# A deformable layer with tiles of 2 by 8 pixels: hats turned once, written to memory and read back as weights

## The chip, the cores and the metric

The kernel runs on one core of a Trainium2 chip. All values are float32. The metric is the device time of one execution in microseconds (us). Before the change three runs took 5849.1, 5850.1 and 5858.9 us; the median is 5850.1.

## The reference

The input x has shape (2, 128, 128, 128): image, channel, row, column. Four layers follow one another, each as x + layer(group_norm(x)): an attention along columns (layer 0), four recurrent scans (layer 1), a deformable convolution (layer 2) and a 4 by 4 Hadamard convolution (layer 3). The change is in layer 2:

```python
out = conv2d(x, w_off, b_off)              # 27 values per pixel
offset = out[:, :18]                       # 9 taps, (y, x)
mask = jax.nn.sigmoid(out[:, 18:])         # 9 taps
py = off_y + ky + hh                       # where tap k reads
px = off_x + kx + ww
sampled = v00*(1-wy)*(1-wx) + v01*(1-wy)*wx + v10*wy*(1-wx) + v11*wy*wx
sampled = sampled * mask
out = einsum('bckhw,ock->bohw', sampled, w) + b
```

So each output pixel reads, for each of 9 taps, the normalised image at a place that is not whole, by bilinear interpolation. The weight of a source pixel at distance (dy, dx) from that place is hat(dy) hat(dx), with hat(d) = max(0, 1 - |d|). A sum over a small window of source pixels, weighted by products of hats, is the same as the interpolation when no offset is larger than the window allows.

## The kernel before

Layer 2 has two stages. `layer2_offsets` (L1123) goes through the images in blocks of 16 rows, 8 per image. For each block it normalises the rows (ACT, L1167), computes the 27 offset and mask channels with 36 products (L1179), turns them so that pixels lie on partitions (om L1187, pt L1195, ot L1199) and writes them to memory as `off_d` (L1203). It also turns the normalised image, so that columns lie on partitions and channels in the free dimension (px L1211, xt L1212), and writes it to memory as `px_d` (L1213), a picture with a border of three pixels of zeros that ACT's queue has written before (L1143, L1148). A last step tests the largest offset: if it is over 2, a slow general way is taken (`layer2_gather`), which does not run here. All engines read that flag and branch (L1116).

`layer2_windows` (L1231) does the sampling. Its unit is a half: 4 rows by 64 columns, 256 pixels, cut into 16 tiles of 4 by 4 pixels. There are 128 halves. A tile's pixels read from a window of 10 by 10 source pixels, which lie on 100 partitions of `xw`, one 128-channel row per tile. The steps for a half:

- `load` (L1253): SP issues ten transfers, one for each window row (L1263), each with 10 columns x 16 tiles x 512 B, and one for the offsets `o` (L1265).
- `hats` (DVE), `hatted` (ACT, absolute value and relu) and `masked` (DVE): for each pixel and tap the ten hats along y and the ten along x, the y ones times the mask.
- `outer` (DVE): for 128 pixels, the products of hats, `w` with 9 taps x 100 places. `turn` (PE): nine transposes of 128 by 100 through the identity, into `ps_w`. `turned` (DVE): copy to `s`, so that each tile has 9 taps x 16 pixels = 144 columns.
- `sample` (PE): eight products for each 128 pixels, `xw` of the tile (100 x 128) with `s` of the tile (100 x 144). A float32 product appears in the trace as two records. `sampled` (ACT): three copies to `sm`.
- `convolve` (PE): nine products with `wdef`, 128 x 128 with 256 columns. `finish` (DVE): adds bias and residual into `res`, and for every second half the statistics of the next norm.

The order on PE, DVE and ACT is the order in which the code calls them: the wrapper `InOrder` (L73) keeps it, so that nearly all of these instructions carry its line, L81. In iteration b of the loop PE runs `turn` of the next 128 pixels, `sample` of these, then `convolve` of the half before (five taps, then four). DVE runs the copy `s`, the outer product for two steps ahead, the hats or the masking for two halves ahead, and `finish`. Loads are asked for three halves ahead, `xw` has four buffers, `ps_w` and `ps_s` one. SP is not wrapped; it issues its transfers one after another, and one that waits holds all that follow.

Of the kernel before, what the change touches and what calls it, by code (L numbers as in the profile page):

```python
# [7 lines left out]
F32 = mybir.dt.float32  # L8
I32 = mybir.dt.int32
AF = mybir.ActivationFunctionType  # L10
ALU = mybir.AluOpType
# [4 lines left out]
P = 128  # L16
N = 2
S = 128
RT = 4
NT = S // RT  # L20
# [4 lines left out]
TP = S + 6  # L25
TE = 131
# [1096 lines left out]
def layer2_offsets(env, prm, res, mem, st_gn, far):  # L1123


    nc, tc = env.nc, env.tc
    ident = env.ident
    NR = 16
    with ExitStack() as ctx:
        cp = ctx.enter_context(tc.tile_pool(name="l2c", bufs=1))  # L1130
# [6 lines left out]
        zero = cp.tile([P, 402], F32, name="zero", tag="zero")  # L1137
        nc.vector.memset(zero, 0.0)
        for n in range(N):
            flat = mem["px"][n].rearrange("y x k -> (y x k)")  # L1140
            for y in (0, S + 3):
                span = 3 * TP * P
                nc.scalar.dma_start(  # L1143
                    out=flat[y * TP * P : y * TP * P + span].rearrange("(p k) -> p k", p=P),
                    in_=zero,
                )
            for c in (0, S + 3):
                nc.scalar.dma_start(  # L1148
                    out=mem["px"][n, 3 : S + 3, c : c + 3, :].rearrange("y x k -> y (x k)"),
                    in_=zero[:, 0 : 3 * P],  # L1150
                )
# [7 lines left out]
        for n in range(N):  # L1159
            for h in range(0, S, NR):  # L1160
# [15 lines left out]
                for k in range(9):  # L1176
# [9 lines left out]
                om = sp.tile([P, 4, RT, 32], F32, name="om", tag="om")  # L1186
                nc.scalar.activation(  # L1187
                    om.rearrange("p b r c -> p r b c"),
                    ps.rearrange("p r (b c) -> p r b c", b=4),
                    AF.Identity,  # L1190
                    bias=boff,
                )
# [15 lines left out]
                for q in range(0, NR, RT):  # L1208
# [4 lines left out]
                nc.sync.dma_start(  # L1213
                    out=mem["px"][n, h + 3 : h + 3 + NR, 3 : S + 3, :].rearrange("y x k -> x y k"),
                    in_=xt,
                )
# [14 lines left out]
def layer2_windows(env, prm, res, mem, st_next):  # L1231
# [3 lines left out]

    nc, tc = env.nc, env.tc
    ident = env.ident
    with ExitStack() as ctx:
# [3 lines left out]
        pe, dve, act = (InOrder(tc, e) for e in (nc.tensor, nc.vector, nc.scalar))  # L1242
# [4 lines left out]
        base = cp.tile([P, 18, 10], F32, name="base", tag="base")  # L1247
        nc.scalar.dma_start(out=base, in_=prm["base2"])

        px = mem["px"]  # L1250
        halves = [(n, g, hf) for n in range(N) for g in range(NT) for hf in range(2)]

        def load(at):  # L1253
            n, g, hf = halves[at]
            xw = sp.tile([100, 16, P], F32, name="xw", tag="xw", bufs=4)
            for y in range(10):
                here = px[n, g * RT + y, hf * 64 : hf * 64 + 10, :]
                src = bass.AP(
                    tensor=here.tensor,
                    offset=here.offset,  # L1260
                    ap=[[P, 10], [4 * P, 16], [1, P]],
                )
                nc.sync.dma_start(out=xw[10 * y : 10 * y + 10], in_=src)  # L1263
            o = sp.tile([P, 2, 27], F32, name="o", tag="o", bufs=4)
            nc.sync.dma_start(out=o, in_=mem["off"][n, g, :, 2 * hf : 2 * hf + 2, :])  # L1265
            return xw, o

        def hats(o):
            d = sp.tile([P, 2, 18, 10], F32, name="d", tag="d")
            dve.tensor_tensor(  # L1270
                d,
                o[:, :, 0:18].unsqueeze(3).to_broadcast([P, 2, 18, 10]),
                base.unsqueeze(1).to_broadcast([P, 2, 18, 10]),
                ALU.add,
            )
            return d

        def hatted(d):
            act.activation(d, d, AF.Abs)
            act.activation(d, d, AF.Relu, bias=1.0, scale=-1.0)  # L1280

        def masked(d, o):
            rows = d.rearrange("p b (k a) s -> p b k a s", a=2)[:, :, :, 0, :]
            dve.tensor_tensor(
                rows, rows, o[:, :, 18:27].unsqueeze(3).to_broadcast([P, 2, 9, 10]), ALU.mult
            )

        def outer(d, b):
            w = sp.tile([P, 9, 10, 10], F32, name="w", tag="w")
            v = d[:, b].rearrange("p (k a) s -> p k a s", a=2)  # L1290
            dve.tensor_tensor(
                w,
                v[:, :, 0, :].unsqueeze(3).to_broadcast([P, 9, 10, 10]),
                v[:, :, 1, :].unsqueeze(2).to_broadcast([P, 9, 10, 10]),
                ALU.mult,
            )
            return w

        def turn(w):
            ps = pp.tile([100, 9, P], F32, name="ps_w", tag="ps_w")  # L1300
            for k in range(9):
                pe.transpose(ps[:, k, :], w[:, k].rearrange("p y x -> p (y x)"), ident)
            return ps

        def turned(ps):

            s = sp.tile([100, 8, 36, 4], F32, name="s", tag="s")
            dve.tensor_copy(
                s.rearrange("p t k c -> p k t c"),
                ps.rearrange("p k (r t c) -> p (k r) t c", r=4, t=8),  # L1310
            )
            return s
# [13 lines left out]
        def sampled(ps, sm, b):  # L1326
            for j in range(3):
                nt = (3, 3, 2)[j]
                lo = 8 * b + 3 * j
                act.copy(  # L1330
                    sm.rearrange("p k (t c) -> p k t c", c=4)[:, :, lo : lo + nt, :],
                    ps[:, j, 0 : nt * 144].rearrange("p (t k c) -> p k t c", t=nt, c=4),
                )

        def convolve(sm, po, taps):
            for k in taps:
                pe.matmul(
                    po,
                    lhsT=wdef[:, k, :],
                    rhs=sm[:, 4 * k : 4 * k + 4, :],  # L1340
                    start=(k == 0),
                    stop=(k == 8),
                )

        def finish(at, po):
            n, g, hf = halves[at]
            here = res[n][:, g * RT : g * RT + RT, hf * 64 : hf * 64 + 64]
            dve.scalar_tensor_tensor(here, po, bdef[:, 0:1], here, ALU.add, ALU.add)
            if hf == 1:
                dve.bn_stats(  # L1350
                    st_next[:, n, g, :],
                    res[n][:, g * RT : g * RT + RT, :].rearrange("p h w -> p (h w)"),
                )

        count = len(halves)
        loads = {at: load(at) for at in range(3)}
        ds = {}
        for at in range(2):  # L1360
            ds[at] = hats(loads[at][1])
            hatted(ds[at])
            masked(ds[at], loads[at][1])
        w = outer(ds[0], 0)
        ps_w = turn(w)
        s = turned(ps_w)
        w = outer(ds[0], 1)
        sms, pos = {}, {}
        for b in range(2 * count + 2):
            at, part = b // 2, b % 2  # L1370
            if part == 0 and at + 3 < count:
                loads[at + 3] = load(at + 3)
            if part == 0 and at < count:
                sms[at] = sp.tile([P, 36, 64], F32, name="sm", tag="sm")


            s_now = s
            if b + 1 < 2 * count:
                ps_w = turn(w)
                s = turned(ps_w)  # L1380
                if b + 2 < 2 * count:
                    w = outer(ds[(b + 2) // 2], b % 2)
            if at + 2 < count:
                if part == 0:
                    ds[at + 2] = hats(loads[at + 2][1])
                else:
                    masked(ds[at + 2], loads[at + 2][1])
            if b < 2 * count:
                ps_s = sample(loads[at][0], s_now, part)
                sampled(ps_s, sms[at], part)  # L1390
                if part == 0 and at + 2 < count:
                    hatted(ds[at + 2])
            if at >= 1:
                if part == 0:
                    pos[at - 1] = pp.tile([P, RT, 64], F32, name="po", tag="po_w", bufs=2)
                convolve(sms[at - 1], pos[at - 1], range(0, 5) if part == 0 else range(5, 9))
                if part == 1:
                    finish(at - 1, pos.pop(at - 1))
                    sms.pop(at - 1), loads.pop(at - 1), ds.pop(at - 1)
# [336 lines left out]
def program(ctx, tc, prm, out):  # L1736
# [16 lines left out]
    mem["px"] = dram.tile([N, TP, TP, P], F32, name="px_d", tag="px_d")  # L1753
# [21 lines left out]
def constants(np):  # L1775
# [27 lines left out]
    pix = np.arange(P)[:, None, None]  # L1803
    at = np.stack(
        [tap // 3 + 2 + pix[:, 0] // 32, tap % 3 + 2 + pix[:, 0] % 4], 2
    ).reshape(P, 18, 1)
    base2 = (at - np.arange(10)).astype(np.float32)
# [94 lines left out]
```

## Time and profile before

| | |
|---|---|
| median of three runs | 5850.1 us |
| the profiled execution | 5858.6 us, its span 5856.4 us |
| mean granted clock of TensorE | 0.965 of full speed |
| PE busy | 5399.6 us (92%) |
| DVE, ACT, POOL busy | 3930.1, 2784.2, 778.5 us |
| layer 2, from its first to its last instruction | about 3910 to 5384 us of the span |
| offsets stage | 3919 to 4091 us |
| windows stage, first load issued to last `finish` | 4098.1 to 5383.6 us |
| memory read and written | 251 and 139 MB |

The span is cut by the profiler into engines: PE (products), PEld (weight loads, which run beside PE), DVE, ACT, POOL and SP, which issues transfers. A line of a timeline has the start and length in us, the engine, the line of the code, the operation, output <- input, shape and count; in brackets stands how long the engine had been idle before it, and what ended that. Groups give a count, busy time in us, the mean of one in ns, and the idle time before them. "DMA share" is the mean busy share of the core's 16 DMA engines, and GB/s is what they moved.

### The profile page before, as it was taken

The page shows a single profiled execution, that of the slowest core. Times are in us where ns is not written, and L with a number is a line of the kernel's source. Part 1 is how long each engine was busy: PE and PEld are TensorE (multiplying, and loading weights), DVE is VectorE, ACT ScalarE, POOL GpSimd, SP SyncE. Part 2 cuts the span into 40 slices and gives each one's busy share as a digit, 9 for nine tenths or more (in the row PEclk, how much of TensorE's full clock was granted, in tenths as well). Part 3 has the DMA queues.
Part 4 walks back from the last instruction along what each step waited for, and adds up shares of the span by engine and source line. Part 5 has one row for each costly group of instructions (what it writes and reads, how often), then busy time and mean ns, then how long its engine had stood idle before and what let it go on. Part 6 is the DMA issues. An engine that isn't in the chain of part 4 may idle for free. (4 is left out here: it accounts for less than half of the span.)

```text
span 5856.4 us, 162646 instructions
## 1 busy us (share of the span) xinstructions
PE 5399.6 (92%) x67323; PEld 4843.0 (83%) x67323; DVE 3930.1 (67%) x7273; ACT 2784.2 (48%) x8408; POOL 778.5 (13%) x727
## 2 busy tenths in 40 slices
PE   8997999999999804999999999999899999998999
PEld 8866777777777704999999999973799999998888
DVE  3646999999999845555555556653566666666887
ACT  1156999999999845443223330012233333333221
POOL 2112333333333221000000003320000000000000
PEclk9998999999999956999999999999899999999999
DMA  3243222222222284000000001114766777663000
GB/s 143 96 192 98 58 61 58 58 57 57 57 59 59 47 344 155 1 2 1 1 1 1 1 1 44 38 45 124 93 88 88 87 87 89 88 88 55 38 39 40
DMA packets 411365, 401.02 MB, mean 68 GB/s; under 512 B 63232, under 2 KB 368256, under 8 KB 397952
## 3 DMA queue, kind: packets, MB, share of 16 engines
q1 hardware_dynamic: 406160, 380.65, 30.6%
q8 instruction: 541, 8.86, 0.7%
q10 hardware_dynamic: 4464, 9.86, 0.5%
q14 instruction: 200, 1.64, 0.1%
HBM read 251.00 MB, written 139.37 MB: 67 GB/s over the span
## 5 line engine op out<-in xcount | busy, mean ns | idle before, releaser
L81 PE MATMUL pl<-ln,wl 128*128 128x128 f32 (+1 forms) x10160 | 1239.0, 276 | 9.0 <-DVE ln L81 8.2
L81 PEld LDWEIGHTS pl<-ln,wl 128*128 128x128 f32 x10160 | 1175.7, 190 | 20.3 <-issue 7.3
L81 ACT ACTIVATE e<-e,mx 128x128 f32<-128x128 f32 x2048 | 793.6, 395 | 0.4 <-DVE mx L81 0.4
L81 ACT COPY sm<-ps_s 128x432 f32<-128x432 f32 (+1 forms) x768 | 318.4, 487 | 817.3 <-PE ps_s L81 817.3
L81 POOL TENSOR_TENSOR e<-e,total 128x1024 f32<-128x1024 f32 x256 | 485.9, 1898 | 1092.2 <-DVE total L81 1092.2
L81 ACT COPY res<-ln 128x128 f32<-128x128 f32 x762 | 262.7, 345 | 720.1 <-DVE ln L81 720.1
L81 DVE COPY s<-ps_w 100x1152 f32<-100x1152 f32 x256 | 346.5, 1354 | 317.7 <-PE ps_w L81 317.7
L81 PE MATMUL ps_s<-s,xw 100*128 100x144 f32 x4096 | 545.2, 286 | 0.4 <-ACT sm L81 0.3
L81 PE MATMUL po<-sm,wdef 128*128 128x256 f32 x2304 | 539.2, 379 | 0.0
L81 PE MATMUL pl<-ln,ws 128*128 128x128 f32 x4064 | 537.1, 273 | 0.0
L81 PEld LDWEIGHTS ps_s<-s,xw 100*128 100x128 f32 x4096 | 517.2, 190 | 0.9 <-ACT sm L81 0.9
L81 DVE TENSOR_TENSOR v<-pl,c 128x128 f32<-128x128 f32 x508 | 148.2, 292 | 542.7 <-PE pl L81 542.7
L81 PEld LDWEIGHTS pl<-ln,ws 128*128 128x128 f32 x4064 | 494.9, 191 | 0.0
L81 PEld LDWEIGHTS po<-sm,wdef 128*128 128x128 f32 x2304 | 419.8, 190 | 47.6
L81 PE MATMUL m<-x,weff 128*128 128x256 f32 x2048 | 444.2, 380 | 14.8 <-DVE x L81 14.8
L81 PEld LDWEIGHTS m<-x,weff 128*128 128x128 f32 x2048 | 390.4, 191 | 68.3 <-issue 14.8
L81 DVE COPY et<-te 128x512 f32<-128x512 f32 x512 | 351.9, 687 | 85.3 <-ACT et L81 84.7
L81 ACT ACTIVATION_READ_ACCUMULATOR e<-e,mx 128x1 f32 x2048 | 397.7, 194 | 0.0
L81 DVE SCALAR_TENSOR_TENSOR ln<-v,res 128x128 f32<-128x128 f32 x1016 | 343.9, 339 | 49.0 <-DVE v L81 1.3
L81 PE MATMUL te<-cst_main,e 128*128 128x128 f32 x2048 | 334.8, 286 | 41.2 <-DVE et L81 33.8
L81 PE MATMUL gen<-zz,toep 32*128 32x128 f32 x8192 | 333.6, 289 | 19.9 <-DMA zz<-qb_d 12.1
L81 DVE TENSOR_SCALAR r<-gen,alphas 128x1024 f32<-128x1024 f32 x256 | 327.1, 1278 | 28.5 <-DMA qk<-qa_d 14.7
(225 smaller groups left out, 8317.6 us busy)
## 6 DMA issues: line engine op xcount, KB each, us to landing
xw<-px_d SPq DMA_DIRECT2D x1280, 80.0 KB
xa<-in_x SPq DMA_DIRECT2D x16, 1024.0 KB
v_d<-vs SPq DMA_DIRECT2D x16, 1024.0 KB
qb_d<-sb SPq DMA_DIRECT2D x16, 1024.0 KB
qa_d<-sa SPq DMA_DIRECT2D x8, 2048.0 KB
zz<-qb_d SPq DMA_DIRECT2D x1024, 16.0 KB
vt<-v_d SPq DMA_DIRECT2D x64, 256.0 KB
qk<-qa_d SPq DMA_DIRECT2D x256, 64.0 KB
```

Of the source, the lines that this page charges most:

```text
L81: return lambda *a, **k: self.tc.keep_in_program_order(issue(*a, **k))
```

## The change

The image in memory gets another form. `px_d` was [image][row][column][channel]; it becomes [image][row][14 places][16 tiles][channel]: for each tile of 8 columns all 14 columns that its window can reach, so that columns near a tile's edge are stored twice. The write of a 16-row block becomes 16 transfers instead of one, because each of the 14 places takes every eighth column.

The unit becomes a strip: 2 rows by 128 columns, 256 pixels, 16 tiles of 2 by 8. A window is 8 rows by 14 columns, 112 partitions of `xw`, which is now read by one transfer with 112 pieces of 8 KB.

Of the 9 taps, 4 go the old way through `outer` and `turn`. For the other 5, the 8 + 14 hats (22 places x 5 taps = 110 columns) of 128 pixels are turned by one transpose (`send`, PE), copied by ACT and written to memory (`hat_d`, two transfers a strip). `receive` reads them back twice: once so that each of the 112 partitions holds the hats of its row (each row's piece repeated for 14 columns), once the hats of its column (each column's piece repeated for 8 rows). DVE multiplies the two (`weights`), which gives the weights of the five taps in place, and copies the other four from PSUM.

`convolve` now runs for each 128 pixels: 9 products with 128 columns instead of 256. SP's transfers in the loop are put in order as well. Offsets are asked for four strips ahead, hats are made three ahead and sent two ahead, the window is read three ahead with three buffers, the two hat tiles two ahead with two buffers.

```diff
+WX, WY = 14, 8
+KW = WX * WY
+PLACES = WX + WY
+TX = S // 8
+TD = 5
...
-                nc.sync.dma_start(
-                    out=mem["px"][n, h + 3 : h + 3 + NR, 3 : S + 3, :].rearrange("y x k -> x y k"),
-                    in_=xt,
-                )
+                to = px_d[n, h + 3 : h + 3 + NR].rearrange("y x t k -> t x y k")
+                nc.sync.dma_start(out=to[0, 3:8], in_=xt[0:5])
+                for j in range(8):
+                    nc.sync.dma_start(out=to[1:TX, j], in_=xt[5 + j : 125 : 8])
+                for j in range(8, WX):
+                    nc.sync.dma_start(out=to[0 : TX - 1, j], in_=xt[j - 3 : 125 : 8])
+                nc.sync.dma_start(out=to[TX - 1, 8:11], in_=xt[125:128])
...
         def load(at):
...
+            xw = sp.tile([KW, TX, P], F32, name="xw", tag="xw", bufs=3)
+            sync.dma_start(
+                out=xw.rearrange("p t k -> p (t k)"),
+                in_=mem["px"][n, y : y + WY].rearrange("y x t k -> x y (t k)"),
+            )
+            return xw
...
+        def send(at, d):
+            ps = pp.tile([PLACES * TD, 2, P], F32, name="ps_h", tag="ps_h")
+            for b in range(2):
+                pe.transpose(ps[:, b, :], d[:, b, 0 : PLACES * TD], ident)
+            ht = sp.tile([PLACES * TD, 2, P], F32, name="ht", tag="ht", bufs=1)
+            act.copy(ht, ps)
+            for b in range(2):
+                sync.dma_start(out=there(at)[:, b], in_=ht[:, b, :])
+
+        def receive(at):
+            got = []
+            src = there(at).rearrange("s b k x -> s (b k x)")
+            for a in range(2):
+                t = sp.tile([KW, 2, TD, P], F32, name=f"hat{a}", tag=f"hat{a}")
+                here = src[0:WY] if a == 0 else src[WY:PLACES]
+                dims = [list(v) for v in here.ap]
+                dims = [[0, WX], dims[0], dims[1]] if a == 0 else [dims[0], [0, WY], dims[1]]
+                sync.dma_start(
+                    out=t.rearrange("p b k x -> p (b k x)"),
+                    in_=bass.AP(tensor=here.tensor, offset=here.offset, ap=dims),
+                )
+                got.append(t)
+            return got
...
-        def turned(ps):
+        def weights(got, b, ps):
+            s = sp.tile([KW, 8, 18, 8], F32, name="s", tag="s")
+            to = s.rearrange("p t k c -> p k t c")
+            row, col = (
+                t[:, b].rearrange("p k (r t c) -> p (k r) t c", r=2, t=8) for t in got
+            )
+            dve.tensor_tensor(to[:, 0 : 2 * TD], row, col, ALU.mult)
             dve.tensor_copy(
+                to[:, 2 * TD : 18], ps.rearrange("p k (r t c) -> p (k r) t c", r=2, t=8)
             )
...
+            if part == 0 and at + 4 < count:
+                offs[at + 4] = load_offsets(at + 4)
...
             s_now = s
             if b + 1 < 2 * count:
+                s = weights(gots[(b + 1) // 2], 1 - part, turn(w))
                 if b + 2 < 2 * count:
+                    w = outer(ds[(b + 2) // 2], part)
+            if part == 0 and at + 2 < count:
+                send(at + 2, ds[at + 2])
+            if part == 0 and at + 3 < count:
+                ds[at + 3] = hats(offs[at + 3])
+            if part == 1 and at + 3 < count:
+                masked(ds[at + 3], offs.pop(at + 3))
             if b < 2 * count:
+                ps_s = sample(xws[at], s_now, part)
+                sms[b] = sampled(ps_s)
+                if part == 0 and at + 3 < count:
+                    hatted(ds[at + 3])
+            if part == 1 and at + 2 < count:
+                gots[at + 2] = receive(at + 2)
+            if part == 1 and at + 3 < count:
+                xws[at + 3] = load(at + 3)
```

The zero border, the table of base places (`base2`), and the shapes of `om` (two ACT operations for one, so that the pixels of a strip lie in the new order) follow the new form.

## The prediction

> **What bounds the kernel now.** I read the busy time by stage first, with the stages cut where layer 2 changes its work. The rows give length, busy time of PE, its weight loads, DVE, ACT and POOL, then the granted clock, the DMA share and GB/s. They are the offsets stage, the way into the windows loop, and the loop.
>
> ```profile
> 3930.00:4090.00 160.00, 158.03 (x1398) 69.06 (x1395) 61.24 (x115) 49.41 (x47) 0.00 (x0) 1.00 0.43 122
> 4098.00:4131.30 33.30, 4.02 (x18) 3.59 (x19) 5.13 (x7) 2.01 (x4) 0.00 (x0) 0.50 0.76 117
> 4131.30:5383.20 1251.90, 1251.37 (x8688) 1173.75 (x8686) 788.82 (x952) 433.03 (x1020) 0.00 (x0) 1.00 0.68 85
> ```
>
> PE is busy for all of the loop's 1251.9 us, at full clock; 128 halves make 9.78 us each. The timeline of PE shows one half, and from layer 1 the pace of 128-column products:
>
> ```profile
> 4703.60 1.89 PE L81 MATMUL po<-sm,wdef 128*128 128x256 f32 x8
> 4705.32 1.15 PE L81 MATMUL ps_w<-cst_main,w 128*100 128x128 f32 x9
> 4706.31 2.13 PE L81 MATMUL ps_s<-s,xw 100*128 100x144 f32 x16
> 4708.27 2.32 PE L81 MATMUL po<-sm,wdef 128*128 128x256 f32 x10
> ...
> 2999.93 2.40 PE L81 MATMUL pl<-ln,wl 128*128 128x128 f32 x20
> 3002.16 1.06 PE L81 MATMUL pl<-ln,ws 128*128 128x128 f32 x8
> ```
>
> From start to start: a turn of one tap takes 0.99/9 = 0.110 us, a sampling record 1.96/16 = 0.1225, a convolution record of 256 columns 0.216, one of 128 columns 2.23/20 = 0.1115. (18 x 0.110 + 32 x 0.1225 + 18 x 0.216 = 9.79.) Next, DVE by shape in the loop, and the transfers as SP issues them:
>
> ```profile
> L81 DVE COPY s<-ps_w 100x1152 f32<-100x1152 f32 x255 | 345.2, 1354 | 315.4 <-PE ps_w L81 315.4
> L81 DVE TENSOR_TENSOR w<-d 128x900 f32<-128x900 f32 x254 | 275.8, 1086 | 0.0
> L81 DVE TENSOR_TENSOR d<-o,base 128x360 f32<-128x360 f32 x126 | 66.5, 527 | 2.3 <-DMA o<-off_d 2.2
> L81 DVE TENSOR_TENSOR d<-d,o 128x180 f32<-128x180 f32 x126 | 43.0, 341 | 0.0
> ...
> 4703.79 4.44 SPq L1263 DMA_DIRECT2D xw<-px_d  x10
> 4708.85 0.34 SPq L1265 DMA_DIRECT2D o<-off_d  x1
> ```
>
> DVE waits for PE, and an SBUF operation of n elements costs 0.155 us + 1.03 ns x n. Last, how fast transfers of different shapes run: the windows xw (10 neighbouring partitions, 512 B pieces), layer 3's weights ta (128 partitions, 8 KB pieces), the px_d writes (128 partitions, 512 B pieces), and the end of a qk load in layer 0 (8 neighbouring partitions, 2 KB pieces).
>
> ```profile
> 4705.00:4713.00 8.00, 8.00 (x60) 7.56 (x59) 5.27 (x7) 2.19 (x6) 0.00 (x0) 1.00 0.81 100
> 5386.00:5388.00 2.00, 0.56 (x2) 0.50 (x2) 1.12 (x7) 0.00 (x0) 0.00 (x0) 0.50 0.96 406
> 3936.00:3938.50 2.50, 2.50 (x32) 0.65 (x25) 0.00 (x0) 0.00 (x0) 0.00 (x0) 1.00 1.04 293
> 1216.50:1218.50 2.00, 1.91 (x35) 1.53 (x39) 1.88 (x3) 2.00 (x11) 0.00 (x0) 1.00 0.46 51
> ...
> 5384.05 0.46 ACTq L1613 DMA_DIRECT2D ta<-in_w  x1
> 5388.91 1.23 DVE L1618 TENSOR_TENSOR tb<-ta 128x1024 f32<-128x1024 f32 x1 [0.49 <-DMA ta<-in_w]
> ```
>
> Pieces of 512 B reach 293 GB/s over 128 partitions, pieces of 2 KB only 51 over 8 neighbours: the spread over partitions sets these rates more than the length of a piece. The loop now asks for 800 KB of xw in 9.78 us and takes some 8 of them at 100 GB/s. It is nearly out of DMA time already, unseen behind PE.
>
> **The change, part by part.** Everything is counted for one strip of 256 pixels, as large as the old half.
>
> PE: 8 turns instead of 18 (0.88), 2 turns of hats (0.22), sampling as before (3.92), the convolution as 36 records of 128 columns (36 x 0.1115 = 4.01). Sum 9.03 us, 0.75 less; over 128 strips -96 us if PE stays the bound.
>
> DVE: four hat additions, 396 elements (4 x 0.155 + 0.41 = 1.03, was 0.53); two maskings, 144 elements (0.46, was 0.34); and twice each: a product of 640 elements (0.81), a copy of 512 from PSUM (0.69 by the 128x512 xt copies), an outer product of 448 (0.62), together 4.24, was 4.88. With the unchanged finish (0.83) 6.56 us, was 6.58: no bound. ACT adds a copy of 256 columns (about 0.37, as layer 0's svt copies) and 36 more elements twice: 4.2 us, was 3.9. Both have over 2 us of each strip free; without that cover they would add nothing until they pass 9.03.
>
> DMA: what is removed is ten xw issues of 80 KB. What comes is one xw of 112 x 8 KB = 918 KB, two hat reads of 112 x 5 KB = 1147 KB in all (each hat piece is read 14 or 8 times over), two hat writes of 56 KB; offsets stay at 27 KB. 2.2 MB per strip in place of 0.83. And they form a chain on SP: the hat writes wait for ACT; the hat reads wait until these writes have landed; the next xw stands behind the hat reads, and the next hat writes' data behind that xw. SP has six issues a strip where it had eleven, so issuing costs nothing; waiting does.
>
> Rate of the reads. Lowest: xw's present 100 GB/s. Highest: ta's 406 scaled to 112 of 128 partitions, 355. In length of pieces the new reads are like ta, in the order of filling (each of 14 columns fills 8 neighbours in turn) like qk and xw. Neither row is nearer, so I take the geometric middle, 188 GB/s: 2.065 MB in 11.0 us (ends 5.8 and 20.7).
>
> Writes of the hats, 113 KB: 0.4 us at 293 GB/s, 1.1 at 100; 0.7. Offsets, 27 KB: 0.1 to 0.3; 0.2. The dead time while SP waits for the write to land and the read starts: ta's issue to its first full microsecond of data takes 1.1 us (5384.05 to 5385.1), end of data to the waiting DVE 0.6 (5388.3 to 5388.9), SP's wake 0.1: 1.8 us, in which nothing else is queued. Cycle: 11.0 + 0.7 + 0.2 + 1.8 = 13.7 us against PE's 9.03. So the hat reads end last, DVE's product waits for them, and PE for DVE; buffers (two for the hats, three for xw) move the wait but don't shorten a cycle that repeats 128 times.
>
> [...]
>
> Offsets stage. A 16-row block writes 218 instead of 128 columns of 8 KB: 1.79 MB in 16 issues, not 1.05 MB in one. Issuing (16 x 0.36 = 5.8 us) is under the block's 10.35. Moving it takes 6.1 us at 293 GB/s (free) to 17.9 at 100; the middle, 171, gives 10.4, with 0.7 for the offsets 11.2: +0.8 x 16 = +13 us (0 to +150), since xt has two buffers. The last block's 15 further issues stand before SP's branch: +5.4 us. om in two ACT operations lets the first turns start earlier; PE waited 2.9 us for it in all, so nothing, -3 at best, +3 if ACT's second start is late. The larger zero fill: +0.3 on DVE, up to +2 on ACT's issues; 1.
>
> Windows stage as a whole, from SP's first issue to the last finish: now 4098.1 to 5383.6, 1285.5 us. After: 10 us to the first hat read (offsets, hats, masks, two sends; xw no longer stands before them as ten issues), 127 cycles of 13.7 = 1740, the last read 7.8, the last strip 11.4, less 10 for the last strips that load nothing further: 1759, +474.
>
> Sum: 474 + 13 + 5 + 1 = +493 on the profiled execution's 5858.6 gives 6352. That execution lies 8.5 us over the median of 5850.1, so against the median 6343, said as 6340. Bounds of the reads alone: cycle 8.5 to 23.5.
>
> **The rivals.** *The reads run wide, and PE stays the bound (faster).* For it: the pieces are long, all 112 partitions are listed, nothing in the rows shows that runs lying apart disturb each other. Then 128 x 9.03 = 1156 + 20 before (33 now, as one xw is issued, not ten) + 2 = 1178 instead of 1285.5: -108, +6 from the offsets stage: about 5750, up to 5840 where the cycle is 9.6 for the dead time. Point of decision: break-even is a cycle of 9.8 us, so 7.1 us for the reads, 290 GB/s. Above that it is faster.
> *Between (slower, but less).* Runs of 8 neighbours disturb each other part of the time, 200 to 280 GB/s, cycles of 10 to 12 us: 5890 to 6130.
> *The reads keep xw's pace (much slower).* 100 GB/s: cycle 23.4, some 7600. Against it: xw fills only 10 neighbours at a time, the new reads 14 runs. The same 5 KB asked for 14 times at once from memory has no row and would push this way.
> *Only the offsets stage pays:* 0 to +150 on top of any of these.
>
> **How the numbers follow.** Reads near the middle (cycle 12 to 15): 0.52, 6125 to 6500. Between: 0.12. Wide: 0.32. Cycles over 15: 0.03. Within 0.2% (about what a measurement of this kernel can tell from no change): 0.01. Slower 0.67, same 0.01, faster 0.32. The likeliest's own range is 6125 to 6500; the range that leaves no more than 2 in 10 out runs from the wide case, 5755, to 6480.
>
> **What would show it.** Right: in the windows stage PE is busy for two thirds, a strip's period is 13 to 14 us, DVE's product waits for the hat tiles from hat_d, SP waits for the hat writes, GB/s is near 160 with a share near one for most of each strip and a gap before each hat read. PE's turns fall to 8 + 2 a strip at 0.110 us, convolution records cost 0.1115. Wrong: PE busy throughout with a period near 9.0 and GB/s near 240; that is the wide case. What would make it wrong is the rate of the two hat reads and xw, and nothing else is as large; next comes the px_d write, where PE idle in the offsets stage would show the +13 too small.

## The result and the profile after

The changed kernel takes 6449.2 us (median of four runs, 6441.4 to 6454.6); the kernel before takes 5852.9 us in runs on the same chip. The ratio is 1.102, with a 95% interval from 1.1003 to 1.1036. The profiled execution of the changed kernel takes 6451.7 us, 593.1 more than that of before (5858.6).

The windows of the changed kernel come first, in the columns that the prediction explained. The first row is the same stretch of the offsets stage as before; the others are the way into the windows loop and the loop.

```profile
3930.00:4090.00 160.00, 141.17 (x1176) 59.77 (x1172) 47.79 (x89) 42.98 (x52) 0.00 (x0) 0.97 0.60 136
4168.20:4206.40 38.20, 17.46 (x110) 15.86 (x111) 15.00 (x41) 9.47 (x22) 0.00 (x0) 0.62 0.66 145
4206.40:5976.40 1770.00, 1368.34 (x9876) 1347.61 (x9874) 799.70 (x1686) 477.98 (x1131) 0.00 (x0) 0.87 0.70 157
```

The windows stage starts at 4168.2, where it started at 4098.1 before: 70 us are lost in the offsets stage. It lasts to 5976.4, 1808.2 us in place of 1285.5: 523 us more. These two make up the 593. PE is idle for 23% of the loop, and its granted clock has gone from 1.00 to 0.87.

The groups of the page name what is waited for (busy time, mean ns of one, then the idle time of that engine just before and what ended it):

```profile
L86 DVE TENSOR_TENSOR s<-hat,hat 112x640 f32<-112x640 f32 x256 | 210.6, 823 | 553.7 <-DMA hat<-hat_d 553.7
L86 PE MATMUL ps_w<-cst_main,w 128*112 128x128 f32 x1024 | 188.8, 316 | 415.0 <-DVE d L86 394.2
L86 ACT COPY ht<-ps_h 110x256 f32<-110x256 f32 x128 | 47.7, 373 | 866.4 <-DMA hat_d<-ht 762.4
```

DVE's product of the two hat tiles waits 553.7 us for the hat reads, and PE's turns wait for DVE. The third line is the other end of the chain: the copy that feeds the hat writes waits for the writes before it. SP's own waits say the same:

```profile
SPq L86 <- DMA hat_d<-ht: 1131.1, 127, 9.9
```

That is 8.9 us in each of 127 strips in which SP stands before a hat read whose hats are not yet in memory. One cycle in the timeline:

```profile
4705.18 1.67 SPq L86 DMA_DIRECT2D hat<-hat_d  x2
...
4706.94 0.80 SPq L86 DMA_DIRECT2D xw<-px_d  x1
...
4707.78 0.54 SPq L86 DMA_DIRECT2D o<-off_d  x1
...
4708.42 1.63 SPq L86 DMA_DIRECT2D hat_d<-ht  x2
...
4713.52 0.82 DVE L86 TENSOR_TENSOR s<-hat,hat 112x640 f32<-112x640 f32 x1 [4.49 <-DMA hat<-hat_d]
...
4718.68 1.67 SPq L86 DMA_DIRECT2D hat<-hat_d  x2
```

All is issued within 4.9 us; then SP waits until 4718.68. The trace's packet records fill in what the queue does meanwhile: pieces of the hat reads move from 4706.8 to 4712.4 (5.6 us), those of xw from 4712.0 to 4717.0 (4.9 us), the last hat write ends at 4717.7, and the first piece of the next hat reads starts at 4720.3. So 10.2 us of reads, 0.75 us of writes after them, and 2.55 us in which nothing large moves. This cycle of 13.5 us is one of the shorter ones. Over 126 strips the packet records give on average 10.9 us from the first piece of the hat reads to the last of xw, 0.5 us of writes after them and 2.56 us until the next hat reads. The mean period, from the first `finish` to the last, is 13.93 us.

In the offsets stage SP's issues have grown, and PE's order has changed. First SP, a block of the kernel before (one px_d issue) and then one of the changed kernel:

```profile
4079.91 0.36 SPq L1213 DMA_DIRECT2D px_d<-xt  x1
...
3949.57 7.10 SPq L1227 DMA_DIRECT2D px_d<-xt  x8
3956.71 5.28 SPq L1229 DMA_DIRECT2D px_d<-xt  x6
3962.03 0.45 SPq L1230 DMA_DIRECT2D px_d<-xt  x1
3962.60 0.40 SPq L1212 DMA_DIRECT2D off_d<-ot  x1
```

An issue of 15 partitions takes 0.88 us, so a block takes SP 13.6 us. The px_d issues run on to 4164.4, 43 us after PE has begun the last of the last block's products. Then PE, again before and changed:

```profile
3994.34 7.97 PE L1179 MATMUL ps_off<-gx,woff 128*32 128x512 f32 x72
4002.25 0.98 PE L1211 MATMUL px<-cst_main,gx 128*128 128x128 f32 x7
4003.18 0.66 PE L1195 MATMUL pt<-cst_main,om 128*128 128x128 f32 x4
4003.68 1.15 PE L1211 MATMUL px<-cst_main,gx 128*128 128x128 f32 x9
...
3990.34 7.95 PE L1187 MATMUL ps_off<-gx,woff 128*32 128x512 f32 x72 [0.73 <-ACT gx L1175]
3998.95 0.81 PE L1204 MATMUL pt<-cst_main,om 128*128 128x128 f32 x4 [0.67 <-ACT om L1196]
3999.59 2.04 PE L1220 MATMUL px<-cst_main,gx 128*128 128x128 f32 x16
4002.55 7.98 PE L1187 MATMUL ps_off<-gx,woff 128*32 128x512 f32 x72 [0.91 <-ACT gx L1175]
```

Before the change 7 of a block's 16 turns of the image (px) stood ahead of the turns of the offsets (pt), and no wait stands in these rows. Now all 16 stand behind them, so that PE waits for `om` and then for `gx`, and a block takes PE at least 12.2 us where it took 10.4.

### The profile page after: what moved, and what is told of

It reads as the page before. It is cut to its first block, busy times and chain, and to the rows that moved or that the text cites. A ratio compares the mean times of both kernels' runs of the same rounds, so it can differ in the third digit from the quotient of the medians.

```text
span 6449.5 us, 165656 instructions
## 1 busy us (share of the span) xinstructions
PE 5543.6 (86%) x68603; PEld 5032.1 (78%) x68603; DVE 3950.2 (61%) x8041; ACT 2837.6 (44%) x8552; POOL 778.3 (12%) x727
## 5 line engine op out<-in xcount | busy, mean ns | idle before, releaser
L86 PE MATMUL ps_s<-s,xw 112*128 112x144 f32 x4096 | 693.9, 335 | 0.5 <-ACT sm L86 0.5
L86 PEld LDWEIGHTS ps_s<-s,xw 112*128 112x128 f32 x4096 | 669.1, 236 | 1.1 <-ACT sm L86 1.1
L86 PE MATMUL po<-sm,wdef 128*128 128x128 f32 x4608 | 566.9, 278 | 0.0
L86 PEld LDWEIGHTS po<-sm,wdef 128*128 128x128 f32 x4608 | 553.4, 196 | 0.0
L86 DVE TENSOR_TENSOR s<-hat,hat 112x640 f32<-112x640 f32 x256 | 210.6, 823 | 553.7 <-DMA hat<-hat_d 553.7
L86 PE MATMUL ps_w<-cst_main,w 128*112 128x128 f32 x1024 | 188.8, 316 | 415.0 <-DVE d L86 394.2
L86 PEld LDWEIGHTS ps_w<-cst_main,w 128*112 128x112 f32 x1024 | 130.7, 152 | 436.1 <-issue 431.7
L86 ACT COPY ht<-ps_h 110x256 f32<-110x256 f32 x128 | 47.7, 373 | 866.4 <-DMA hat_d<-ht 762.4
```

The source lines that it names most:

```text
L86: return lambda *a, **k: self.tc.keep_in_program_order(issue(*a, **k))
```

## The experiments

The open questions were why the reads run at 190 GB/s (2.065 MB in 10.9 us), what the order on SP costs, and where the 70 us of the offsets stage come from. The packet records gave a first hint: a piece of 8 KB takes 309 ns (median) in layer 3's `ta`, which fills 128 partitions, and 618 ns in the new xw. Pieces of 5 KB take 358 ns where the fastest take 194. This table holds the medians for all kernels below, over the stretch from 4400 to 5300 us:

```
kernel                       8 KB (xw), ns   5 KB (hats), ns   strip, us   time, us
changed kernel                    618              358           13.93      6449.2
e1   9 rows                       309              196           15.19      6615.0
e2   writes earlier               549              333           10.14      5971.3
e3   16 partitions                618              356           13.94      6415.0
e4   e1 + e2 + e3                 309              196           13.39      6369.0
e5   9 rows, writes by places     312              196           10.93      6072.6
e6   e5 + e2 + e3                 309              218           10.28      5959.0
e7   e3, two queues               619              358           13.90      6477.5
e8   e6 + masks first             345              229            9.53      5840.1
e9   e8 + order of offsets        358              232            9.43      5808.1
e10  xw as 16 runs of 8           615              358           14.00      6450.5
e11  e9 with 8 rows               528              313            9.71      5873.8
```

In runs beside these the kernel before took 5848 to 5853 us (medians).

**e1: nine rows.**

```diff
-TP = S + 6
-WX, WY = 14, 8
+TP = S + 7
+WX, WY = 14, 9
...
-            o = sp.tile([P, 2, 27], F32, name="o", tag="o", bufs=3)
+            o = sp.tile([P, 2, 27], F32, name="o", tag="o", bufs=2)
...
```

The zero fill grows by a row. To make room, `o` has two buffers in place of three and a small tile of layer 0 is given back. Two theories were set against each other. Theory A, runs in step, was the author's guess that runs of 8 partitions filled side by side hold each other up and runs of 9 don't. It gave packets of xw near 309 ns, 6.3 to 9.4 us of reads, a strip of 10 to 13 us and a time of 5960 to 6360 us. Theory B is a rate of bytes.

> The changed kernel with windows of nine rows in place of eight: 14 x 9 = 126 partitions, five hats of 23 in place of 22 places, xw 14 x 9 x 8 KB = 1032 KB and the two hat reads 1290 KB, so 12.5% more bytes; the ninth row has weight zero for all offsets the branch admits, so the result is the same. In the changed kernel's trace a strip takes 13.8 us: hat reads 5.6 us of data, xw 4.9, hat writes 0.9, offsets 0.5, the rest nothing moving. Its 8 KB packets of xw take 609 ns (median of the packet records) where layer 3's ta, also 8 KB packets, takes 309. [...] Theory B (a rate of bytes: the same pieces asked for many times, or 14 engines' own pace): time goes as the bytes, 10.5 x 1.125 = 11.8 us, a strip 15.1, the kernel 6449 + 128 x 1.3 = 6615 us, packets of xw unchanged at about 609 ns.

The time is 6615.0 us, to the microsecond what the theory of bytes had said, and yet that theory fell: the packets went from 618 to 309 ns and from 358 to 196, as the theory of runs in step had said. In one cycle the hat reads took 4.7 us and xw 3.4, 12.5% more bytes in less time. What took the gain, and 1.3 us more, is another transfer:

```profile
4713.51 1.73 SPq L86 DMA_DIRECT2D hat<-hat_d  x2
4715.34 0.79 SPq L86 DMA_DIRECT2D xw<-px_d  x1
4716.22 0.51 SPq L86 DMA_DIRECT2D o<-off_d  x1
4716.83 6.25 SPq L86 DMA_DIRECT2D hat_d<-ht  x2
```

The issue of the two hat writes takes 6.25 us in place of 1.63, and their 230 pieces end 23.6 ns apart, over 5.42 us, where 220 pieces took 0.8 to 0.9. With nine rows a write is listed by 23 places, with eight by 22. The packet records show what differs: for 4.6 of the 5.4 us exactly one of these pieces is in flight, and never more than two, while of the changed kernel's 220, in the cycle shown, four or more are for 89% of the time. For most of its time xw has 14 in flight here and in the changed kernel, and `ta` has 16. That the number 23 is the cause was the author's estimate, which e5 tries. A total that hits a forecast is no evidence while its parts were not looked at.

**e2: hat writes a strip earlier.**

```diff
...
-            if part == 0 and at + 2 < count:
-                send(at + 2, ds[at + 2])
...
             if part == 1 and at + 2 < count:
                 gots[at + 2] = receive(at + 2)
             if part == 1 and at + 3 < count:
+                send(at + 3, ds[at + 3])
                 xws[at + 3] = load(at + 3)
```

> The changed kernel with the hat writes one strip earlier: strip k+3's hats are turned, copied and written behind the hat reads of strip k+2 and ahead of its xw load, so that these writes land while xw is loaded, and the next hat reads find them there. Bytes, issues and buffers are as before. Theory A (dead time): the 2.5 us of a cycle between the end of the hat writes' data and the first data of the hat reads go; a strip is reads 10.5 + writes 0.9 + offsets 0.5 with little between, 11.3 to 12 us in place of 13.8; 127 x (1.8 to 2.5) = 230 to 320 us less, 6130 to 6220. Rival B (the wait is worth nothing: the queue's own issue and start latency stand in any order, or the writes slow the xw load by what they save): 6420 to 6460.

5971.3 us, 478 less: the theory's direction, and about 160 us beyond its range. A strip takes 10.14 us. SP's timeline:

```profile
4713.61 1.66 SPq L86 DMA_DIRECT2D hat<-hat_d  x2
4716.78 1.61 SPq L86 DMA_DIRECT2D hat_d<-ht  x2
4718.44 0.83 SPq L86 DMA_DIRECT2D xw<-px_d  x1
...
4723.91 1.66 SPq L86 DMA_DIRECT2D hat<-hat_d  x2
```

The next hat reads are issued 5.5 us after xw, while xw is still moving (its pieces run from 4721.1 to 4727.1, the hats' from 4715.3 to 4722.4). So not only the 2.55 us go: each transfer now runs into the next one, and DMA share rises from 0.70 to 0.88. DVE's wait for the hat reads has left the first places of the loop's waits, and another stands there:

```profile
PE ps_h L86 <- DVE d L86: 115.5, 124, 2.0
```

PE waits 0.9 us a strip for the masked hats that it is to turn, because `send` moved ahead in PE's order and `masked` stayed behind three long operations in DVE's. SP now waits for ACT's copy `ht` behind these turns (291 us in all), so the transfers wait for the engines and no longer only for each other.

**e3: 16 partitions per px_d issue.**

```diff
-mem["px"] = dram.tile([N, TP, WX, TX, P], ...)
+mem["px"] = dram.tile([N, TP, WX, TX + 2, P], ...)
...
-nc.sync.dma_start(out=to[0, 3:8], in_=xt[0:5])
-for j in range(8): ... in_=xt[5 + j : 125 : 8]
-for j in range(8, WX): ... in_=xt[j - 3 : 125 : 8]
-nc.sync.dma_start(out=to[TX - 1, 8:11], in_=xt[125:128])
+for j in range(WX):
+    t = 2 if j < 3 else 0 if j > 10 else 1
+    nc.sync.dma_start(out=to[t : t + TX, j], in_=xt[(j - 3) % 8 : 128 : 8])
```

> The changed kernel with px_d of 18 in place of 16 tile columns, two of them outside the image, so that each of the 14 columns of a tile is written by one issue of 16 partitions in place of 15 (14 issues for a block in place of 16, 1.84 MB in place of 1.79; the windows read the same 16 tile columns). In the changed kernel an issue of 15 partitions holds SP 0.84 to 0.88 us, one of 5 or 3 partitions 0.37 to 0.45, and the 128-partition write of the kernel before 0.34 to 0.37; the px_d writes run from 3935.1 to 4164.0. Theory A (issue time bounds the offsets stage: 14 x 0.86 + 1.2 = 13.2 us for a block, plus waits, over PE's 10.35): if 16 partitions are issued in 0.35 to 0.4 us, a block issues in 5.3 us, and the stage ends 45 to 65 us earlier; the kernel 6385 to 6405 us. Rival B (moving bounds it: 14.3 us for 1.79 MB is 125 GB/s, and the pieces of 512 B are as many): issues may be short, the stage keeps its 225 to 235 us, the kernel 6440 to 6460 us. Rival C (an issue costs by its descriptors, not by its number of partitions): 14 issues of 0.9 us, 12.6 us a block, at most 15 us off the kernel.

6415.0 us, 34 less: outside all three ranges, between the first two. The issues got shorter, not short:

```profile
3996.70 9.38 SPq L1227 DMA_DIRECT2D px_d<-xt  x14
4006.17 0.57 SPq L1212 DMA_DIRECT2D off_d<-ot  x1
4008.91 9.50 SPq L1227 DMA_DIRECT2D px_d<-xt  x14
```

14 issues take 9.4 us, 0.67 each. SP now waits 2.2 us in each block, and the block is PE's 12.2 us. So SP's issues were one cause in this stage; the waits for `om` and `gx` in PE's order stand behind it as a second, which e9 tries.

**e4: e1, e2 and e3 together.**

> Nine rows, the earlier hat writes and the 16-partition px_d writes together. By theory A of all three a strip's transfers take 6.3 to 9.4 us for the reads + 0.9 + 0.5 = 7.7 to 10.8 us against PE's 9.03 us: windows stage 1180 to 1400 us in place of 1808, offsets stage 45 to 65 us less, the kernel 5770 to 5990 us: at the lower end faster than the kernel of ten xw issues (5850). By the rivals: nine rows add 128 x 1.3 = 166 us, the earlier writes save nothing, 6580 to 6620 us. If nine rows fail and the other two hold: 6449 + 166 - 275 - 55 = about 6285 us.

6369.0 us, a miss. A strip takes 13.39 us: the hat writes, again 5.4 us with one piece in flight, stand between the two reads.

**e5: e1 with hat writes of 16 and 7 places.** A strip's hats are stored as [place][tap][row][half][64], pieces of 1 KB.

```diff
-for b in range(2):
-    sync.dma_start(out=there(at)[:, b], in_=ht[:, b, :])
+for lo, hi in ((0, 16), (16, PLACES)):
+    sync.dma_start(out=there(at)[lo:hi], in_=ht[TD * lo : TD * hi] ...)
```

> [...] Here each strip's hats are kept with a place's two halves side by side (pieces of 1 KB) and written in two issues, 16 places and 7. Theory A (runs in step halve the reads, and one engine's writes hid it in e1): hat writes 0.5 to 1.0 us, a strip 15.2 - 4.5 = 10.3 to 11.5 us, the kernel 5990 to 6150 us. Rival (the writes are slow for another reason, such as the 115 partitions or the reads beside them): a strip 14 to 15.2 us, 6460 to 6615 us.

6072.6 us and 10.93 us a strip, inside the theory's range. The hat write takes 0.7 us in one cycle, the reads keep their 312 and 196 ns. Against the changed kernel the rows, what made room for them and the form of the hat writes differ, and 377 us are gone although more bytes are read.

**e6: e5 with e2 and e3.**

> e5 with the earlier hat writes of e2 and the 16-partition px_d writes of e3. Theory: reads 7.8 us, writes 0.5 to 1.0 and offsets 0.5, one after the other without dead time 8.8 to 9.3 us a strip, which meets PE's 9.03 us (4.01 convolution + 3.92 sampling + 1.10 turns): windows stage 1180 to 1240 us in place of 1808, offsets stage 34 us less as e3 showed: 5780 to 5850 us, so faster than the kernel of ten xw issues by up to 1.2%. Rival (issue time on SP, 4.6 us, and waits of SP in its order keep the transfers apart): a strip 10 to 10.5 us as in e2, 5920 to 5990 us.

5959.0 us and 10.28 us a strip: the rival's range. Against e4 the form of the hat writes alone makes 410 us. But e2's strip with eight rows, 10.14 us, was no longer: its wait is here too (us in total, times and longest), and faster reads are worth nothing behind it:

```profile
PE ps_h L86 <- DVE d L86: 125.4, 124, 1.4
```

**e7: px_d writes on two queues**, e3 with `(nc.sync, nc.scalar)[j % 2].dma_start(...)`.

> e3 with the 14 px_d issues of a block dealt in turn to SP's queue and ACT's. In e3 14 issues of 16 partitions take 9.1 to 10.3 us of SP, 0.65 to 0.74 each, and a block 12.2 us where PE alone needs 10.35. If the issue time of one queue bounds the block: SP 7 x 0.7 + 0.6 = 5.5 us, ACT 3.3 + 4.9 = 8.2 us, both under 10.35, the px_d stage ends some 25 to 30 us earlier and the kernel takes 6380 to 6392 us in place of 6415. If one generator behind both queues, or the moving of 512 B pieces, bounds it: 6405 to 6425 us, issues on either queue at 1.2 to 1.4 us. If ACT's issues hold up its own work (om, gx): slower than e3, up to 6450.

6477.5 us, 62 slower than e3: the third case, and worse than its bound.

```profile
4003.16 6.30 ACTq L1227 DMA_DIRECT2D px_d<-xt  x6
...
4009.50 4.40 ACT L1175 ACTIVATE gx<-res,gb_l,gs_l 128x2304 f32<-128x2304 f32 x2 [6.04 <-DMA px_d<-xt]
4011.86 10.69 PE L1187 MATMUL ps_off<-gx,woff 128*32 128x512 f32 x72 [9.47 <-ACT gx L1175]
```

ACT spends 6.3 us on issues before it makes `gx`, and PE stands still for 9.5 us. ACT's six issues take 1.05 us each here; over the stage an issue takes 0.94 us on ACT's queue and 0.97 on SP's, longer than the 0.65 of e3's one queue, while both together move mostly 200 to 280 GB/s in place of about 195.

**e8: e6 with the masks first on DVE.**

```diff
             s_now = s
+            if part == 1 and at + 3 < count:
+                masked(ds[at + 3], offs.pop(at + 3))
             if b + 1 < 2 * count:
                 s = weights(gots[(b + 1) // 2], 1 - part, turn(w))
...
-            if part == 1 and at + 3 < count:
-                masked(ds[at + 3], offs.pop(at + 3))
```

> e6 with one move on DVE: the masking of strip k+3's row hats stands at the start of a strip's second half, ahead of the hat products and the outer product, not behind them. In e6 a strip takes 10.2 us; in 112 of them PE waits for DVE's d before the hat turns, 1.0 us each, and the hat write and the next xw issue stand behind these turns (the write is issued 0.6 us after them, at 4710.51, xw at 4711.97), so that the transfers stand still for about 1.8 us from 4711.7 to 4713.6. Theory (the wait for the masked hats sets the pace): turns start 1.0 to 1.4 us earlier, a strip 9.1 to 9.5 us, the kernel 5959 - 127 x (0.7 to 1.1) = 5820 to 5870 us. Rival (transfers take 10 us a strip in any order, hat reads and xw running into each other: both ran 5.3 us in e6): within 10 us of e6, 5950 to 5970 us.

5840.1 us, inside the theory's range; the ratio to the kernel before is 0.9988 (0.9973 to 1.0003), no difference that can be told. A strip takes 9.53 us (in the profiled execution, which was 24 us over the median), and PE's wait for `d` is gone from the list of waits.

**e9: e8 with a fixed order in the offsets stage.** The edit is given in outline, with what stays in brackets. SP's `off_d` write also moves behind the px_d writes.

```diff
+pe, dve, act = (InOrder(tc, e) for e in (nc.tensor, nc.vector, nc.scalar))
 (offset products, om)
+turned(0); turned(RT); turned(2 * RT)      # 12 px turns
 (pt: four turns of om)
+turned(3 * RT)                             # the last four
 (ot, most, sigmoid)
+norm(at + 2)                               # gx of block k+2
```

> e8 with the offsets stage written in a fixed order on PE, DVE and ACT: a block's first 12 px turns stand between its offset products and its offset turns (which wait for the two om operations), and gx of block k+2 behind om of block k. In the kernel before, px turns stood there too and PE never waited; in the changed kernel and in e3 all 16 px turns stand behind the offset turns, PE waits 0.66 us for om and 0.91 us for gx in each block, and a block takes 12.2 us in place of 10.4. Theory: about 1.6 to 1.9 us of each of 16 blocks go, as long as SP's 14 issues (9.1 to 10.3 us) and 0.55 for the offsets stay under 10.4: 20 to 30 us less than e8. Rival (SP's issues or the moving of px_d at 190 GB/s, 1.84 MB in 9.7 us + 0.7, set the block): at most 8 us less, as the block can't go under 11.5 us.

5808.1 us, 32 less than e8, where 20 to 30 were expected; e8's runs scatter from 5825 to 5875 us and e9's from 5797 to 5825. PE's order in the trace:

```profile
3996.80 7.97 PE L86 MATMUL ps_off<-gx,woff 128*32 128x512 f32 x72
4004.70 1.53 PE L86 MATMUL px<-cst_main,gx 128*128 128x128 f32 x12
4006.07 0.60 PE L86 MATMUL pt<-cst_main,om 128*128 128x128 f32 x4
4006.50 0.60 PE L86 MATMUL px<-cst_main,gx 128*128 128x128 f32 x4
4007.03 7.95 PE L86 MATMUL ps_off<-gx,woff 128*32 128x512 f32 x72
```

No waits, and a block takes 10.2 us, less than before the change. The last px_d issue starts at 4092.6 (4131.4 in e8, 4164.0 in the changed kernel, 4090.3 before), and the windows stage starts at 4098.3 (4132.7 in e3, 4168.2 in the changed kernel, 4098.1 before): the 70 us of this stage are gone. This version beats both kernels, the one before by 0.7%: its ratio to the kernel before is 0.9931, with an interval from 0.9915 to 0.9947. Its windows loop:

```profile
4139.60:5337.50 1197.90, 1158.62 (x9876) 1147.77 (x9874) 838.17 (x1686) 472.66 (x1130) 0.00 (x0) 1.00 0.83 258
```

PE is busy for 97% at full clock: 1158.6/127 = 9.12 us a strip.

**e10: xw as 16 runs of 8**, on 128 partitions; the products use 112 of them. The question is whether the slow packets come from the runs of 8 or from the 112 partitions.

```diff
-xw = sp.tile([KW, TX, P], ...)
+xw = sp.tile([16 * WY, TX, P], ...)
...
-in_=mem["px"][n, y : y + WY].rearrange("y x t k -> x y (t k)"),
+in_=bass.AP(...),                         # 16 columns of 8 rows
...
-lhsT=xw[:, 8 * b + t, :],
+lhsT=xw[0:KW, 8 * b + t, :],
```

> The changed kernel with xw loaded as 16 columns of 8 rows in place of 14, 128 partitions, 1049 KB in place of 918; the products still use the first 112, the hats are untouched, and px_d has one more row of zeros. [...] Theory A (runs in step hold each other up): packets of 8 KB stay near 609 ns, xw takes 4.9 to 5.1 us of data although it carries 14% more, the kernel 6430 to 6470 us. Rival (14 engines or 112 partitions are the cause): packets near 309 ns, xw 2.5 to 3.2 us, 127 x 1.9 less, 6170 to 6250 us. Rival (a rate of bytes): packets as before, xw 5.6 us, 6449 + 127 x 0.7 = 6540 us.

6450.5 us, 1.3 from the changed kernel, and packets of 615 ns: the theory of runs in step. The transfer now has the partitions and the pieces of `ta`, whose packets take 309 ns, and is only listed in another way. With e1 this excludes the bytes, the repeated reads and the 14 pieces in flight (e1 has the last two as well), and the 112 partitions. In the changed kernel nearly all pieces of xw are slow: 0.3% take under 340 ns. So the runs show that packets take double time in runs of 8 side by side (618 ns in the changed kernel, 615 in e10) and not in runs of 9 (309 in e1); which partitions disturb each other was not tried and stays open.

**e11: e9 with eight rows.**

> e9 with windows of eight rows again, everything else kept (the hat writes now in 16 and 6 places); 11% fewer bytes to read than e9. Theory A: with runs of 8 in step the reads take 10.2 us a strip, as in the changed kernel (5.6 + 4.9, overlapping by 0.3) and as e2's strip of 10.14 us, and set the pace: 5808 + 127 x (10.0 to 10.2 - 9.43) = 5880 to 5905 us, packets of xw near 600 ns, PE waiting for the hat products. Rival (the order alone made e9 fast, and nine rows are worth nothing once the transfers are queued without gaps): a strip 9.3 to 9.5 us, 5790 to 5815 us.

5873.8 us: neither range, a little under the first. A strip takes 9.71 us, so the theory was wrong to take the changed kernel's reads (10.2 us in the cycle shown, 10.9 on average) as a fixed price: with hat reads and xw running into each other the packets come down to 528 and 313 ns. In the profiled executions nine rows are worth 0.28 us a strip; the medians lie 66 us apart, but that of e11 scatters by 34 us and its profiled execution was its fastest, so the worth of the ninth row is 0.6 to 1.1%.

## Why the prediction was right, and where it was off

The forecast was slower by 490 us; it was slower by 596 (599 against 5850.1, from which the forecast was counted). Its case, a chain of transfers on SP that ends later than PE, is what the profile shows. By its own steps:

- *Rate of the reads, 188 GB/s, 11.0 us.* They took 10.9 us on average, 189 GB/s: the term held. It was reached as the geometric middle of two far rows, 100 and 355 GB/s, and that this middle was met is luck. What slowed the reads e1 and e10 show: an 8 KB piece of xw takes 618 and 615 ns in runs of 8, 309 in runs of 9.
- *Writes 0.7, offsets 0.2.* 0.5 us on average after the end of xw; the offsets run beside it.
- *Dead time 1.8 us.* 2.56 on average. The working took one issue, one landing and a wake. No run shows the wake's 0.1 us by itself; in the cycle shown, between the last write's end at 4717.7 and SP's next issue lies 1.0 us, and another 1.6 to the first piece.
- *Cycle 13.7 us.* 13.93; 127 x 0.23 = 29 us. The dead time was 0.8 us too short, and the writes and offsets 0.4 too long, which hid half of it. What the step did not see is that the dead time was not the only price of the order: e2, which takes only the wait away, gained 3.8 us a strip.
- *Start and end of the windows stage, 19 us outside the cycles (10 + 7.8 + 11.4 - 10).* 1808.2 - 127 x 13.93 = 39: 20 us missed.
- *Offsets stage +13 and its end +5, with 1 for the zero fill.* +70: the largest miss, 51 us. The step that failed is "Issuing (16 x 0.36 = 5.8 us) is under the block's 10.35". The 0.36 us came from an issue of 128 partitions; one of 15 takes 0.88, so issuing was the bound and its 43 us of backlog stood before the branch. e3 took 34 us of it. The other part is the step on `om`, costed at nothing: PE's order changed with it, and e9, which puts the order back, gained 32. With both, the windows stage starts when it did before the change. Whether the two `om` operations or the longer issues led to that order was not separated.
- *PE 9.03 us.* In e9, where PE is the bound, 1158.6/127 = 9.12. *DVE 6.56, ACT 4.2, no bounds.* 799.7 and 478.0 us of the loop are 6.30 and 3.76 a strip. DVE's sum came out although a part of it did not: the outer product of 448 elements took 0.94 us, not 0.62, while operations that follow one another overlap in the trace: the copy at 4714.26 starts 0.08 us before the end of the product that began at 4713.52 and took 0.82.

The missed 100 us are these: 29 + 20 + 51.

Of the signs that it named, the period of 13 to 14 us, the waits of DVE and SP, 157 GB/s and the gap before each hat read came true. The DMA share was to be near one for most of each strip; it averages 0.70. PE was to be busy for two thirds; it is busy for 77%, as its clock fell to 0.87 and a sampling burst after a wait took 3.11 us (4717.22) and the next one 2.13.

The "between" case did not fit its own sum: 200 GB/s and the sum's other terms make a cycle of 13.0 us, not 12. The wide case, faster by about 100 us, failed at the rate of the reads (189 GB/s where break-even was 290). The runs show how near it was: PE's saving is real, and with the hat writes earlier and in two issues by places, the masks first and the offsets stage put right, eight rows come to 5873.8 and nine to 5808.1.

## What to carry to other kernels

Before a load is turned into one long transfer, see how its listing deals partitions out: a write by 23 places had one piece in flight here, a read by 14 columns 14, and an 8 KB piece took 618 ns in runs of 8 partitions filled side by side, 309 in runs of 9. A write that is read back should go out a whole step before its read, with another transfer in between; that order was worth 3.8 us of a 13.9 us step here, more than the 0.75 us of arithmetic that the change saved. The price of an issue is to be taken from a transfer of the same shape (0.36 us for 128 partitions here, 0.88 for 15), and where a forecast total comes out exact, as in e1, its parts are to be looked at before it is believed.

## What the runs showed that was not expected

- Hat writes listed by 23 places ran 5.42 us for 230 pieces, by 22 places 0.8 to 0.9 us for 220, by 16 and 7 about 0.7.
- SP's issue time: 0.36 us for 128 partitions, 0.88 for 15, 0.65 for 16, and for the same load of `o` 0.34 us in the kernel before and 0.54 in the changed one. What sets it stays open.
- One queue moved the 512 B pieces of px_d at about 195 GB/s, two queues mostly at 200 to 280; the stage was still slower, as the second queue was ACT's.
- A PE that waits 3 us in each strip was granted 0.87 of its clock, and 1.00 again in e2, where it waited 0.9 us.
